# Moving the load, negation and accumulating load of one weight sum from unit 7 to unit 3 of a twenty-unit product schedule

## The chip, the cores and the metric

The kernel runs on one core of a Trainium2 chip. The metric is device time in microseconds (us) of one execution. The engines are TensorE (PE in the profile, with its weight loads as PEld), VectorE (DVE), ScalarE (ACT), GpSimd (POOL) and SyncE (SP); transfers are issued from SP, ACT and POOL.

## The reference, cut to what matters

`x` has 2708 rows of 1024 float32 values, `adj` is a 0/1 matrix of 2708 by 2708 in which a row has about four ones. One layer is computed:

```python
h = jnp.maximum(_layernorm(x, axis=-1), 0.0)
q = h @ W_q.T + b_q
k = h @ W_k.T + b_k
v = h @ W_v.T + b_v
z = (1 / sqrt(1024)) * (q @ k.T)
spare_z = z * adj
spare_z = jnp.where(spare_z == 0.0, -10000.0, spare_z)
attn = softmax(spare_z, axis=1)
x = x + relu(attn @ v)
```

## The kernel before, in words

**The algebra.** The kernel forms M = W_q.T W_k (scaled) once, and then needs only two products per row tile of 128 rows: `h M` (in place of the query), and `u W_v` where `u` is the weighted sum of the few rows of `h` that a row's neighbours name. Both products go in pairs of row tiles through a scheme of seven block products in place of eight. The 2 by 2 blocks of a 1024 by 1024 matrix lie in the tile `M[:, i, j]`, and sums of them in `T[:, 0..3]` (a view of `wlow`).

**The units.** There are twenty units, run in order by `multiply(n, ...)`: units 0 to 9 (kind "q") multiply by M, units 10 to 19 (kind "o") by W_v; one row tile (the last in `order`) is left for a single product at the end. `FIRST` is 4, `last_q` is 9. A unit has 28 matmuls of 512 columns, each shown as two instructions. Inside a unit, `after(i)` with i from 0 to 6 is called between the products, and everything else of the kernel is hung on these places: the steps written out in `steps_at` (a key (3, 5) is place 5 of unit 3), the next unit's operands, and the attention. The last two products of unit n lie on either side of `between(n)`, which calls `opened(n + 1)`: the first two products of the next unit and the copies `psy<-ps` (L1024) and `p<-ps` (L1029) of their sums on ScalarE. `u2` (L1060) is ScalarE's copy of the next sum.

**The blocks of M and of W_v.** In q units the first product that takes `s1` uses `T[:, 0]`, in o units `M[:, 0, 1]`. So `M[:, 0, 1]` (called `t1` in `after`) is free from the moment when the sums `T` and the squares of M are formed. It is to hold a sum of W_v for the o units: block (0, 0) of W_v is loaded into it, ScalarE negates it in two instructions, and an accumulating load on GpSimd's queue adds block (0, 1). At place 3 of unit 9 VectorE reads it for `T[:, 1]`.

**The squares.** `squared(k)` (L375) lets ScalarE sum the squares of M's block k, for a flag that chooses a general path after the main one. Steps `g0` to `g3` are the four blocks, `g4` is the bias row. Block 1 is `M[:, 0, 1]`.

**The neighbour table.** Each row's neighbours are found by VectorE and sorted by their count. `put` (steps `w`, L626) writes the table's rows in the sorted order to DRAM by one indirect transfer per row tile from GpSimd; `reload` (step `b`) brings them back. `w0-7` at (3, 6) writes the eight tiles that the attention takes first. `o0`, in `opened(4)`, sorts them (`pos_i`, L689).

**The attention.** From unit 4 on VectorE works a stream of scores (L863) and weighted sums (L923) over rows that GpSimd gathers by indirect transfers (`g<-h_dram`, L610; `pq`, L612). Its steps alternate by hand with what VectorE does for the units.

**What sets the order.** Up to the start of unit 4 the order on ScalarE and VectorE is as written (`manual_schedule`), from unit 4 on only that of VectorE; GpSimd, SP and TensorE are ordered by the compiler's planner, which lets an instruction go early when its inputs allow it. `tc.issue_after(ins)` puts what a block issues behind `ins` on that engine's queue. `load_rows` gathers the rows of a unit (`qr<-h_dram`, L612). `banks_for` (L760) puts the bias row into two accumulators.

Of the kernel before, what the change touches and what calls it, by code (L numbers as in the profile page):

```python
# [14 lines left out]
AF = mybir.ActivationFunctionType  # L15
ALU = mybir.AluOpType
AX = mybir.AxisListType

P = 128
NB = 512  # L20
# [3 lines left out]
SLOTS = 16  # L24
# [41 lines left out]
def tile_preln_masked_attention(  # L66
# [12 lines left out]
    nc = tc.nc  # L79
# [3 lines left out]
    scale = 1.0 / math.sqrt(D)  # L83
# [26 lines left out]
    h_dram = dram.tile([N, D], FT, name="h_dram")  # L110
# [65 lines left out]
    t = 0  # L176
    while t < NT:
# [4 lines left out]
        t = e  # L182
# [58 lines left out]
    def moments(t):  # L241

        group, xs, mv = next(g for g in normed.values() if t in g[0])
        i = t - group[0]
        junk = work.tile([P, D], mybir.dt.uint8, tag="junk", name="junk_x", bufs=1)
        nc.scalar.activation(junk, xs[i], AF.Copy, scale=-1.0 / (ROOT * D), accum_out=mv[:, i, 0:1])
        nc.scalar.activation(junk, xs[i], AF.Square, scale=1.0 / ROOT, bias=mv[:, i, 0:1], accum_out=mv[:, i, 1:2])
# [61 lines left out]
    def follow(steps):  # L309

        for step in steps.split():
            first, *only = step[1:].split(".")
            first, *last = first.split("-")
            first = int(first or 0)
            if step[0] == "s":
                stats(range(first, int(last[0] if last else first) + 1))
            elif step[0] == "m":
                moments(first)
            elif step[0] == "r":
                root(first)  # L320
            elif step[0] == "a":
                apply(first, *[range(int(o[0]), int(o[-1]) + 1) for o in only])
            elif step[0] in "hk":
                keep(first, step[0] == "h")
            elif step[0] == "+":
                owe(first)
            elif step[0] == "p":
                counted(first)
            elif step[0] == "c":
                counts(*halves[first])  # L330
            elif step[0] == "o":
                sorted_at.append(sort(*halves[first]))
            elif step[0] == "w":
                pooled.close()
                with tc.issue_after((behind if first < EARLY else products)[-1].ins):
                    entered.append(put(first, int(last[0]) + 1))
            elif step == "z":
                pooled.enter_context(tc.manual_schedule(engines={mybir.EngineType.Pool}))
                with tc.issue_after(entered[-1].ins):
                    reload(EARLY, NT)  # L340
            elif step[0] == "b":
                reload(*halves[first])
            elif step[0] == "g":
                squared(first)
            else:
                if step[0] == "e":
                    counted(first)
                if step[0] != "j":
                    found(first, *[range(int(o[0]), int(o[-1]) + 1) for o in only])
                if step[0] != "i":  # L350
                    listed(first)
# [94 lines left out]
    with tc.tile_pool(name="w", bufs=1, side="left") as wp:  # L446
# [11 lines left out]
        t1 = [work.tile([P, D], FT, tag="hT", name=f"t1_{k}", bufs=2) for k in range(2)]  # L458
# [49 lines left out]
        Y = [psum.tile([P, NB], FT, tag="tp", name=f"ps_y{i}") for i in range(H)]  # L508
# [98 lines left out]
    def gather(dst, src, t, w, n, skip=False):  # L607
        off = bass.IndirectOffsetOnAxis(ap=ptab.bitcast(U32)[:n, t, w:w + 1], axis=0)
        if skip:
            return nc.gpsimd.indirect_dma_start(out=dst, out_offset=None, in_=src, in_offset=off,  # L610
                                                bounds_check=N - 1, oob_is_err=False)
        return nc.gpsimd.indirect_dma_start(out=dst, out_offset=None, in_=src, in_offset=off)  # L612

    rows_of = {}
    FIRST = EARLY // 2
# [136 lines left out]

    placed = []

    def banks_for(row):

        return_ = []
        for h in range(NH):
            return_.append(psum.tile([P, NB], FT, tag="acc", name=f"ps{h}"))
            nc.scalar.copy(return_[h], row[:, h * NB:(h + 1) * NB])  # L760
        return return_

    def natural_rows(n):
# [23 lines left out]
    steps_ahead = {(1, 5): "o1"}  # L787

    slots, free = [], []
# [1 line left out]
    def searched():  # L791
        search.close()

        att = ph.enter_context(tc.tile_pool(name="att", bufs=1, side="right", reuse_waits="tile"))
        for i in range(HIGH):
            slots.append(att.tile([P, D], FT, name=f"g{i}"))

        assert len(adj_loads) == NT
# [210 lines left out]
    def add_block(bank, a, b, last=True):  # L1009
        for c in range(4):  # L1010
            mm = nc.tensor.matmul(bank, a[:, c, :], b[:, c, :], start=False, stop=(c == 3), skip_group_check=True)  # L1011
        return mm
# [3 lines left out]
    def opened(n):  # L1016

        if n not in banks_of:
            return
        X, Z = banks_of[n]  # L1020
        ops = ops_of[n][0]
        add_block(X, ops["a11"], M[:, 0, 0])
        Y = psum.tile([P, NB], FT, tag="acc", name="psy")
        nc.scalar.copy(Y, X)  # L1024
        if n == FIRST:
            follow("o0")
        products.append(add_block(Z, ops["s1"], T[:, 0] if units[n][0] == "q" else M[:, 0, 1]))
        p5 = small("p5")
        nc.scalar.copy(p5, Z)  # L1029
        opened_of[n] = Y, p5  # L1030

    def between(n):

# [16 lines left out]
    def multiply(n, results, after):  # L1050


        X, Z = banks_of.pop(n)
        ops = ops_of.pop(n)[0]
        Y, p5 = opened_of.pop(n)
        after(0)
        after(1)
        products.append(add_block(Y, ops["s2"], T[:, 1]))
        u2 = small("u2")
        nc.scalar.copy(u2, Y)  # L1060
        after(2)
        add_block(X, ops["a12"], M[:, 1, 0])
        results[0](X)
        after(3)
        products.append(add_block(Z, ops["s4"], M[:, 1, 1]))
        results[2](Z, u2)
        after(4)
        products.append(add_block(Y, ops["s3"], T[:, 2]))
        results[1](Y, p5)
        after(5)  # L1070
        between(n)
        add_block(Y, ops["a22"], T[:, 3])
        results[3](Y)
        after(6)
# [119 lines left out]
    def of_wv(i, j):  # L1194

        return wv[j][:, i * 4:(i + 1) * 4, :]
# [7 lines left out]
    def load_rows(unit):  # L1204
        kind, *pair = unit
        rows = []
        for t in pair:
            if t in held:
                rows.append(held.pop(t))
                continue  # L1210
            rows.append(row_tile(f"{kind}r_{t}"))
            if kind == "q":
                gather(rows[-1], h_dram[:, :], t, SLOTS, P)
            else:
                assert t in done, (t, done)
                if t in faced_tiles:
                    by_quarters(rows[-1], u_dram[t * P:(t + 1) * P, :])
                else:
                    nc.sync.dma_start(rows[-1], u_dram[t * P:(t + 1) * P, :])
        return rows  # L1220

    products = []
    last_q = len(q_pairs) - 1
# [13 lines left out]
    for n, unit in enumerate(units):  # L1237
# [15 lines left out]
        def after(i):  # L1253
# [15 lines left out]
                    with tc.issue_after(sorted_at[-1].ins):  # L1269
                        nc.vector.memset(g, 0.0)  # L1270
            b11, t1, b21, b22 = M[:, 0, 0], M[:, 0, 1], M[:, 1, 0], M[:, 1, 1]
            for at, place, src in (((-2, 0), t1, of_wv(0, 0)), ((0, 3), b21, of_wv(1, 0))):
                if (n - last_q, i) == at:
                    nc.sync.dma_start(place, src)
            if (n - last_q, i) == (0, 4):
                for h in range(2):
                    nc.scalar.copy(b22[:, 2 * h:2 * h + 2], T[:, 0, 2 * h:2 * h + 2])
            if (n - last_q, i) == (-2, 6):
                for h in range(2):
                    nc.scalar.activation(t1[:, 2 * h:2 * h + 2], t1[:, 2 * h:2 * h + 2], AF.Copy, scale=-1.0)  # L1280
                nc.gpsimd.dma_start(t1, of_wv(0, 1), accum_op=ALU.add)
            for at, place, a, b in (((0, 3), T[:, 1], T[:, 0], t1), ((1, 0), T[:, 2], T[:, 1], b11),
                                    ((1, 1), T[:, 3], b21, T[:, 1])):
                if (n - last_q, i) == at:
# [40 lines left out]
                follow(steps_at[n, i])  # L1325
            if (n, i) == (3, 4):
                searched()
            if (n, i) == (3, 6):
                for s in range(8, HIGH):
                    for c in range(0, D, D // 4):  # L1330
                        with tc.issue_after(entered[-1].ins):
                            nc.gpsimd.memset(slots[s][:, c:c + D // 4], 0.0)
# [70 lines left out]
    with tc.If(some > 0):  # L1403
# [19 lines left out]
        with tc.tile_pool(name="big", bufs=1, side="right") as big, tc.tile_pool(  # L1423
# [34 lines left out]
            with tc.For_i(0, NT) as i:  # L1458
                r0 = nc.snap(smin(i * P, N - P))
                rows = bass.ds(r0, P)  # L1460
# [119 lines left out]
```

## Time and profile before

| What | Before |
|---|---|
| time, median of 3 runs | 630.61 us (629.04 to 632.04) |
| time of the profiled execution | 627.51 us |
| its span, first to last instruction | 625.8 us, at a mean granted TensorE clock of 0.999 |
| TensorE | 618.9 us busy, 99% of the span |
| VectorE | 526.4 us, 84% |
| GpSimd | 366.9 us, 59% |
| ScalarE | 290.4 us, 46% |
| weight loads of TensorE | 310.0 us, 50% |
| transfers | 183.24 MB, 293 GB/s on average |

How to read it: shares are over the whole span, and the stages differ. The first 107 us form M, the normed rows and the neighbour lists, units 0 to 3 run to about 217 us beside the search, and the attention begins at about 239 us. A row of the timeline gives start, duration, engine, line, operation, output and input, and in square brackets the idle time of the engine just before it and what ended it. POOLq, SPq and ACTq are the issues of transfers in an engine's queue.

### The profile page before, as it was taken

To read this page: it belongs to the slowest core of one execution; us is meant where nothing else is said; L and a number is where in the kernel's file an instruction comes from. 1 tells how busy PE (TensorE), PEld (TensorE's weight loads), DVE (VectorE), ACT (ScalarE), POOL (GpSimd) and SP (SyncE) were. 2 spreads that over 40 slices of the span, in tenths; PEclk is the share of its full clock that TensorE was granted. 3 is DMA by queue.
4 is the path that set the end of the run, shared out by engine and by line. 5 is a ranking of instruction groups with operands and counts; after the bars stand their busy time and mean duration, and the time that the engine had idled before them with its cause. 6 is when DMAs were issued, how large, how long until landed. Compare 5 with 4: busy or idle time off the path is not lost.

```text
span 625.8 us, 6069 instructions
## 1 busy us (share of the span) xinstructions
PE 618.9 (99%) x1571; PEld 310.0 (50%) x1571; DVE 526.4 (84%) x1024; ACT 290.4 (46%) x421; POOL 366.9 (59%) x394
## 2 busy tenths in 40 slices
PE   9999999999999999999999999999999999999996
PEld 5777767444444444444444444444444444444442
DVE  5999878988988947979898998999988899898541
ACT  3538985749677372433331532443442433432300
POOL 2649870786668577856654342767577657752421
PEclk9999999999999999999999999999999999999999
DMA  8999998688797559997696999999999999995571
GB/s 331 407 369 323 340 356 317 211 265 322 251 369 278 171 166 364 349 321 250 212 374 193 368 340 311 282 332 328 347 341 343 335 306 340 293 293 139 149 254 71
DMA packets 65952, 183.24 MB, mean 293 GB/s; under 512 B 10055, under 2 KB 20631, under 8 KB 65272
## 3 DMA queue, kind: packets, MB, share of 16 engines
q0 software_dynamic: 26656, 86.02, 43.8%
q1 hardware_dynamic: 32026, 71.53, 32.7%
q10 hardware_dynamic: 7230, 25.25, 10.4%
q8 instruction: 14, 0.23, 0.1%
q14 instruction: 26, 0.21, 0.1%
HBM read 147.23 MB, written 43.88 MB: 305 GB/s over the span
## 4 chain that ended last, share of the span: by engine, by line
PE 99%; POOL 0%; DVE 0%; POOLq 0%; issue 0%
PE ps L1011 46%; PE psy L1011 33%; PE ps_y L476 7%; PE ps_x L476 4%; PE ps_z L476 4%; PE pt L415 3%; PE ps_y L511 1%; PE ps_h L1230 0%; PE ps_v L594 0%; DVE y_alone L1396 0%; POOL out_dram L1380 0%; POOLq L1402 0%; POOL hsum L121 0%; PE ps_in L678 0%; PE ps_all L680 0%
## 5 line engine op out<-in xcount | busy, mean ns | idle before, releaser
L610 POOL DMA_INDIRECT g<-h_dram,tab x93 | 120.0, 1290 | 60.6 <-issue 20.0
L1011 PE MATMUL ps<-M,a 128*128 128x512 f32 x320 | 144.0, 593 | 0.0
L1011 PE MATMUL psy<-wlow,s 128*128 128x512 f32 x320 | 143.9, 592 | 0.0
L863 DVE SCALAR_TENSOR_TENSOR junk<-g,pq 128x1024 uint8<-128x1024 f32 x92 | 112.3, 1220 | 9.6 <-DMA g<-h_dram,tab 7.9
L1011 PE MATMUL ps<-M,s 128*128 128x512 f32 x240 | 107.9, 592 | 0.0
L1011 PEld LDWEIGHTS ps<-M,a 128*128 128x128 f32 x320 | 60.0, 190 | 72.2 <-issue 71.3
L1011 PEld LDWEIGHTS psy<-wlow,s 128*128 128x128 f32 x320 | 60.0, 190 | 72.1 <-issue 70.6
L923 DVE SCALAR_TENSOR_TENSOR u<-g,coef,u 128x1024 f32<-128x1024 f32 x70 | 89.8, 1283 | 7.0 <-ACT u L912 5.6
L389 DVE FIND_INDEX8 at<-ones,adj 128x8 uint32<-128x685 f32 (+1 forms) x88 | 74.5, 864 | 0.0
L1011 PEld LDWEIGHTS ps<-M,s 128*128 128x128 f32 x240 | 45.5, 190 | 57.2 <-issue 56.5
L1011 PE MATMUL psy<-wlow,a 128*128 128x512 f32 x160 | 72.0, 593 | 0.0
L368 ACT ACTIVATE sized<-adj 128x2708 uint8<-128x2708 f32 (+1 forms) x22 | 54.2, 2466 | 7.3 <-DMA adj<-in_adj_dram 6.0
L298 POOL TENSOR_TENSOR hsum<-hsum,x 128x256 f32<-128x256 f32 (+1 forms) x56 | 38.7, 732 | 26.5 <-DVE wlow L444 22.4
L1115 POOL DMA_INDIRECT y<-in_x_dram,tab x19 | 32.6, 1714 | 32.2 <-ACT y L1132 16.6
L1011 PEld LDWEIGHTS psy<-wlow,a 128*128 128x128 f32 x160 | 30.3, 190 | 38.6 <-issue 37.1
L808 POOL DMA_INDIRECT out_dram<-y,tab x21 | 27.0, 1284 | 16.0 <-issue 13.9
L1011 PE MATMUL ps<-wlow,s 128*128 128x512 f32 x80 | 36.1, 593 | 0.0
L944 ACT COPY v<-u 128x1024 f32<-128x1024 f32 x20 | 20.9, 1044 | 32.3 <-DVE u L923 24.8
L912 ACT ACTIVATE u<-g,coef 128x1024 f32<-128x1024 f32 x16 | 18.4, 1148 | 28.8 <-DVE coef L911 23.5
L626 POOL DMA_INDIRECT tab_dram<-tab,pos_i x22 | 21.6, 982 | 13.7 <-DVE pos_i L689 8.2
L276 ACT ACTIVATE x<-x,r 128x1024 f32<-128x1024 f32 (+1 forms) x22 | 25.8, 1232 | 5.1 <-POOL r L266 5.1
L760 ACT COPY ps<-bp_sb 128x512 f32<-128x512 f32 x42 | 24.6, 595 | 7.7 <-DVE y L1150 7.0
(253 smaller groups left out, 841.1 us busy)
## 6 DMA issues: line engine op xcount, KB each, us to landing
adj<-in_adj_dram SPq DMA_DIRECT2D x21, 1354.0 KB, 11.1
x<-in_x_dram SPq DMA_DIRECT2D x21, 512.0 KB, 11.0
h_dram<-x ACTq DMA_DIRECT2D x21, 512.0 KB, 7.2
u_dram<-v ACTq DMA_DIRECT2D x20, 512.0 KB, 7.3
or<-u_dram SPq DMA_DIRECT2D x80, 128.0 KB, 10.0
q_late<-q SPq DMA_DIRECT2D x12, 512.0 KB, 5.6
pq<-q_late POOLq DMA_DIRECT2D x12, 512.0 KB, 10.2
M<-in_wv_dram SPq DMA_DIRECT2D x3, 1024.0 KB, 15.9
```

The costliest lines, as they stand in the source:

```text
L276: nc.scalar.activation(xs[i][:n], xs[i][:n], AF.Relu, bias=r[:n, 4, i:i + 1], scale=r[:n, 3, i:i + 1])
L298: small.append(nc.gpsimd.tensor_add(hsum[:n, cols], hsum[:n, cols], xt[:n, cols]))
L368: nc.scalar.activation(sized[:n], a[:n, :, :PW], AF.Abs, accum_out=total[:n, t:t + 1])
L389: nc.vector.max_index(at[:n, k - first_k, g, :], ones[:n, 0:8], a[:n, g, :])
L476: mm = nc.tensor.matmul(bank, a_tile(o + H * a[0], a[1], i), b(o), start=first and o == 0, stop=(o == H - 1), skip_group_check=True)
L610: return nc.gpsimd.indirect_dma_start(out=dst, out_offset=None, in_=src, in_offset=off, bounds_check=N - 1, oob_is_err=False)
L760: nc.scalar.copy(return_[h], row[:, h * NB:(h + 1) * NB])
L808: to = nc.gpsimd.indirect_dma_start(out=out, out_offset=bass.IndirectOffsetOnAxis(ap=ptab.bitcast(U32)[:n, t, SLOTS:SLOTS + 1], axis=0), i ...
L863: chained(lambda: nc.vector.scalar_tensor_tensor(junk, g_of[t][s], 1.0, tq[t], op0=ALU.mult, op1=ALU.mult, accum_out=zall[:, t, s:s + 1]))
L923: chained(lambda: nc.vector.scalar_tensor_tensor(u, g_of[t][s], coef[:, s:s + 1], u, op0=ALU.mult, op1=ALU.add))
L1011: mm = nc.tensor.matmul(bank, a[:, c, :], b[:, c, :], start=False, stop=(c == 3), skip_group_check=True)
L1115: return nc.gpsimd.indirect_dma_start(out=y[:n], out_offset=None, in_=x, in_offset=off, compute_op=ALU.add)
```

## The change

The three steps on `t1` that stood at (7, 0) and (7, 6) go to unit 3. The load of block (0, 0) is issued by ScalarE at (3, 2), behind its copy `u2` of unit 3, in place of SP. The negation stands at (3, 5), behind ScalarE's copies for the accumulators, and the accumulating load of block (0, 1) is issued by GpSimd behind the latest gather of `load_rows`, which is written ahead of the puts `w0-7` at (3, 6). So that the block is free by then, its squares (`g1`) go from (3, 6) into `opened(3)`, behind the copy `p5`; `g0` goes from (3, 5) to (3, 6). The lists `bank_at`, `rows_at` and `copied_at` only keep the instructions for `issue_after`. Nothing else is changed; no arithmetic is added or removed.

```diff
@@ banks_for
+    bank_at, rows_at, copied_at = [], [], []
-            nc.scalar.copy(return_[h], row[:, h * NB:(h + 1) * NB])
+            bank_at.append(nc.scalar.copy(return_[h], row[:, h * NB:(h + 1) * NB]))
@@ steps_at
-                (3, 1): "i21", (3, 3): "p21", (3, 4): "j21 c0", (3, 5): "g0", (3, 6): "w0-7 g1 g2 g3 g4", (4, 4): "b0"}
+                (3, 1): "i21", (3, 3): "p21", (3, 4): "j21 c0", (3, 6): "w0-7 g0 g2 g3 g4", (4, 4): "b0"}
@@ opened(n), behind the copy p5
+        if n == FIRST - 1:
+            follow("g1")
@@ multiply
-        nc.scalar.copy(u2, Y)
+        copied_at.append(nc.scalar.copy(u2, Y))
@@ load_rows
-                gather(rows[-1], h_dram[:, :], t, SLOTS, P)
+                rows_at.append(gather(rows[-1], h_dram[:, :], t, SLOTS, P))
@@ after(i)
-            for at, place, src in (((-2, 0), t1, of_wv(0, 0)), ((0, 3), b21, of_wv(1, 0))):
-                if (n - last_q, i) == at:
-                    nc.sync.dma_start(place, src)
+            if (n - last_q, i) == (0, 3):
+                nc.sync.dma_start(b21, of_wv(1, 0))
...
-            if (n - last_q, i) == (-2, 6):
-                for h in range(2):
-                    nc.scalar.activation(t1[:, 2 * h:2 * h + 2], t1[:, 2 * h:2 * h + 2], AF.Copy, scale=-1.0)
-                nc.gpsimd.dma_start(t1, of_wv(0, 1), accum_op=ALU.add)
...
+            if (n, i) == (3, 2):
+                with tc.issue_after(copied_at[-1].ins):
+                    nc.scalar.dma_start(t1, of_wv(0, 0))
+            if (n, i) == (3, 5):
+                with tc.issue_after(bank_at[-1].ins):
+                    for h in range(2):
+                        nc.scalar.activation(t1[:, 2 * h:2 * h + 2], t1[:, 2 * h:2 * h + 2], AF.Copy, scale=-1.0)
+                with tc.issue_after(rows_at[-1].ins):
+                    nc.gpsimd.dma_start(t1, of_wv(0, 1), accum_op=ALU.add)
```

## The prediction

> **What bounds the kernel now.** I read the page's head first, then the waits of TensorE, then the chain that ended last, and at the end the timelines of each queue around units 3 and 4.
>
> ```profile
> span 625.8 us, 6069 instructions
> PE 618.9 (99%) x1571; PEld 310.0 (50%) x1571; DVE 526.4 (84%) x1024; ACT 290.4 (46%) x421; POOL 366.9 (59%) x394
> PE 99%; POOL 0%; DVE 0%; POOLq 0%; issue 0%
> ```
>
> TensorE is busy for 618.9 of 625.8 us, and the chain that ended last is TensorE alone. The next fences show where the other 6.9 us lie: first three stretches of the span (each engine's busy time and instructions, clock, share of the transfer engines, GB/s), then all waits of TensorE (total, times, longest), then pieces of the chain (start, duration, instructions).
>
> ```profile
> 1.20:620.00 618.80, 618.80 (x1571) 309.95 (x1571) 525.49 (x1023) 290.35 (x421) 365.31 (x388) 1.00 0.88 295
> 620.00:625.80 5.80, 0.08 (x1) 0.00 (x0) 0.69 (x1) 0.00 (x0) 0.96 (x1) 0.88 0.24 90
> ```
>
> ```profile
> PE ps_y L511 <- POOL hsum L121: 1.2, 1, 1.2
> ```
>
> ```profile
> 187.39 6.87 PE psy L1011 x16
> 209.87 3.59 PE ps L1011 x8
> 368.13 7.08 PE psy L1011 x16
> 592.39 6.87 PE ps L1011 x16
> ```
>
> TensorE's only wait is the 1.2 us before its first instruction. From 1.20 to 620.00 us it has no idle time, and the 5.8 us behind it are the last addition and scatter, which the change does not touch. The chain's pieces say that this busy time is not waiting in disguise: 16 instructions take 6.87 us (0.43 us each) at 187 us as at 592 us; the slow pieces are 209.87 (3.59 for 8, where 3.44 is the rule) and 368.13 (7.08 for 16), some 0.1 to 0.2 us each. The granted clock in the first stretch is 1.00. So the kernel is as long as TensorE's own instructions, and an edit that leaves those alone can gain a few tenths of a us. It can lose only where it makes TensorE wait. That is the question for each part: how late may what it moves become before TensorE stands still?
>
> **The change part by part.** The rows for ScalarE, which carries most of it (start, duration, what, and idle time before it):
>
> ```profile
> 187.43 0.58 ACT L1029 COPY p<-ps 128x512 f32<-128x512 f32 x1 [1.35 <-PE ps L1011]
> 190.86 0.58 ACT L1105 COPY q<-psy 128x512 f32<-128x512 f32 x1 [2.85 <-PE psy L1011]
> 196.40 0.57 ACT L1060 COPY u<-psy 128x512 f32<-128x512 f32 x1
> 197.73 0.58 ACT L1094 COPY q<-ps 128x512 f32<-128x512 f32 x1 [0.77 <-PE ps L1011]
> ...
> 205.91 0.58 ACT L718 COPY a<-pt 128x512 f32<-128x512 f32 x1 [3.14 <-PE pt L415]
> 206.39 1.06 ACT L375 ACTIVATE junk_m<-M 128x1024 uint8<-128x1024 f32 x1
> ...
> 208.54 0.19 ACT L375 ACTIVATION_READ_ACCUMULATOR junk_m<-M 128x1 f32 x1
> 209.78 0.57 ACT L1024 COPY psy<-ps 128x512 f32<-128x512 f32 x1 [1.06 <-PE ps L1011]
> ...
> 231.97 2.00 ACT L1280 ACTIVATE M<-M 128x1024 f32<-128x1024 f32 x2 [3.76 <-DMA M<-in_wv_dram]
> 233.88 0.57 ACT L1081 COPY taken<-psy 128x512 f32<-128x512 f32 x1
> ...
> 250.75 0.33 ACTq L946 DMA_DIRECT2D u_dram<-v  x1
> ```
>
> 1. *Squares of block 1* (`g1`). Their cost is that of `g0`, from 206.39 to 208.73 (208.54 + 0.19): 2.34 us. They go behind `p<-ps`, which ends at 188.01, ahead of `q<-psy`, which waits 2.85 us for TensorE until 190.86. 188.01 + 2.34 = 190.35, so they lie wholly in that gap, with 0.5 us to spare. Cost 0. Without the cover, 2.34 us would fall on the copy of a result, which nobody needs at once.
>
> 2. *Issue of the load by ScalarE.* An issue of ScalarE's queue took 0.33 us, the same load by SP 0.52 us (its row below). It stands behind `u<-psy`, which ends at 196.97, in a gap of 0.77 us. By either price it fits. Cost 0; the load starts at about 197.0. On SP it goes away at 226.56, where the next store stands behind it; nobody on the chain waits for that store.
>
> 3. *The negation* costs 2.00 us (row 231.97) and takes the place of `g0`, 2.34 us, at 206.39; `g0` goes to the four squares at (3, 6), whose number stays (`g1` left them). So ScalarE's load there falls by 0.34 us, if the block has landed by 206.39. Behind the negation stands `psy<-ps` at 209.78, and behind that all of ScalarE: this is the wait that the change adds. Landing is bounded by these rows:
>
> ```profile
> 225.44 0.38 SPq L638 DMA_DIRECT2D tab<-tab_dram  x1
> ...
> 226.56 0.52 SPq L1274 DMA_DIRECT2D M<-in_wv_dram  x1
> ```
>
> ```profile
> DMA to landing us min/median/max: 12.3/14.1/15.9
> ```
>
> ```profile
> q0 software_dynamic: 208, 0.73, 56.4%
> ```
>
> ```profile
> 201.00:202.00 1.00, 1.00 (x10) 1.00 (x9) 0.78 (x2) 1.00 (x3) 1.00 (x2) 1.00 0.00 0
> ```
>
> The same megabyte, issued at 226.56, let the negation go at 231.97: 5.4 us. The slowest landing of any transfer into M took 15.9 us (second fence, min, median, max). From 197.0 that is 202.4 or 212.9. I take 202.4 and a little: in the four us from 197 the gathers' queue moves only 0.73 MB (third fence: packets, MB, share), and from 201 to 202 us the transfer engines do nothing at all (fourth: share 0.00), so 1 MB has room. I put the landing at 203, 3 us ahead of need. [...] The upper bound is rival A.
>
> The load also shares the transfer engines with the two gathers for unit 4, issued from 193.51 on, whose rows TensorE turns at these times:
>
> ```profile
> 200.96 1.04 PE L415 MATMUL pt<-ident,qr 128*128 128x128 f32 x8
> ...
> 205.27 1.04 PE L415 MATMUL pt<-ident,qr 128*128 128x128 f32 x8
> ...
> 217.60 3.60 PE L1011 MATMUL psy<-wlow,s 128*128 128x512 f32 x8
> ```
>
> Both gathers are in by 201 (share 0.00 from there). The first is half of their 1 MB and, being first in its queue, is nearly through when the load's first bytes come; the second may lose some 2 us, and has from about 200.5 to 205.27. Cost 0; without the cover, up to 2 us of TensorE.
>
> 4. *The accumulating load* on GpSimd's queue, and the queue that it is moved past:
>
> ```profile
> 208.13 1.06 POOL L612 DMA_INDIRECT qr<-h_dram,tab  x1 [0.31 <-issue]
> 214.30 1.01 POOL L626 DMA_INDIRECT tab_dram<-tab,pos_i  x1 [5.12 <-DVE pos_i L689]
> ...
> 223.28 0.97 POOL L626 DMA_INDIRECT tab_dram<-tab,pos_i  x1 [0.30 <-issue]
> ...
> 228.78 0.99 POOL L612 DMA_INDIRECT pq<-q_dram,tab  x1 [1.43 <-DMA tab<-tab_dram]
> ...
> 258.54 1.02 POOL L1281 DMA_DIRECT2D M<-in_wv_dram  x1
> ```
>
> It takes 1.02 us and 0.3 between issues. GpSimd stands idle for 5.12 us before the first put, which waits for VectorE's `pos_i`; the negation ends at about 208.4, the last gather at 209.19, so the issue is over by about 210.5, 3.8 us before 214.30. Cost 0, and 1.3 us less among the gathers at 258. In the shared queue its data go ahead of the puts'. It landed 12.3 us after issue among gathers (the minimum above); from 209.5 that gives 221.8, before the last put is even issued (223.28). So the reload at 225.44 stays where it is; if the data took as much again, the reload and the attention would be about 8 us later (233.8 less 225.4).
>
> 5. *What becomes better at 226 to 270 us.* The load's 1 MB leaves the engines just when the first `pq` and `g` gathers are asked for, and ScalarE no longer stands 3.76 us in front of `taken`. VectorE gets its first score sooner:
>
> ```profile
> 238.87 1.23 DVE L863 SCALAR_TENSOR_TENSOR junk<-g,pq 128x1024 uint8<-128x1024 f32 x1 [3.47 <-DMA g<-h_dram,tab]
> ...
> 252.25 1.28 DVE L722 TENSOR_TENSOR s<-a,pt 128x512 f32<-128x512 f32 x2 [1.06 <-ACT a L718]
> ```
>
> ```profile
> 261.43 3.60 PE L1011 MATMUL ps<-wlow,s 128*128 128x512 f32 x8
> ```
>
> The gathers may come 1 to 3 us earlier (at most the 3.47 us that the first score waited). But even now what VectorE makes at 252.25 is used by TensorE at 261.43, about 8 us after the first of the pair is done. Nothing on the chain waits for the attention, so the gain is put at 0.
>
> The sum: 0 + 0 + 0 + 0 + 0 = 0 on the profiled execution's 627.51 us (625.8 of span and 1.7 around it). That execution lies 3.1 us under the median of 630.61; my forecast is the median unchanged, 630.6, of itself 629.0 to 632.0 as the runs shown spread. What a measurement of this kernel tells from no change is about 0.5%, 3.15 us.
>
> **The rivals.**
>
> *A. The load comes late and TensorE waits (slower).* Place: ScalarE's queue at 206.39, where the negation holds up `psy<-ps`. That copy opens the sum to which TensorE adds at 217.60. With 2.00 for the negation and 0.57 for the copy, it decides from a landing at 215.0 on, 18 us after issue; from there each us costs one. For it: in this stage no load has been issued from ScalarE's queue before, the gathers share the engines, and two of three such transfers needed 12.3 and 15.9 us. Against it: even 15.9 leaves 2.1 us. If the delay were 24 us (half as much again as 15.9), the stall would be 5.9 us: 636.5.
>
> *B. TensorE's busy time hides waits (faster).* [...] Against it stands the even 0.43 us per instruction, early and late, which bounds the gain within the profile by about 1 us. What the profile can't exclude is that the 3.1 us between it and the median are such waits in the gathering stage; if all went, the time would be 627.5.
>
> *C. The change doesn't do what it says.* GpSimd is ordered by the planner; it may let the puts pass if it reckons the negation late. Then the accumulating load comes at about 224, among or behind the puts, and issue 1.3 us is added before `pq`. Against the 8 us at 252.25 this is nothing: 630.6 too.
>
> **How the numbers follow.** No change to the chain: 0.76. C: 0.05, the same time. A: 0.12, the margins being 2 us at the worst row and 12 us at the likeliest, but the order of a whole stage is moved. B: 0.07. Faster by over 0.5% only if B takes all of the 3.1 us, 0.07; within 0.5%: 0.81; slower: 0.12. The range goes down to B's 627.5 and up into A as far as a stall of about 4 us, 634.5, which leaves out A's longer stalls and lesser odds.
>
> **What would show it.** Right: TensorE again with the one wait of 1.2 us and 618.9 us; squares of one block at about 188; the load from ScalarE's queue at 197; the negation at 206 to 209 with no wait for a transfer before it; the accumulating load at about 209.5, the first put still at 214.3 and the reload at about 225.4; the first score at 236 to 239. Wrong: a wait of ScalarE for `M<-in_wv_dram` that runs past 215, TensorE waiting for `psy` at 217 or for `qr` at 201, puts that start after 216, or a TensorE whose busy time falls.

## The result, and the profile after

| What | Before | After |
|---|---|---|
| time, median of 22 runs each | 629.93 us (628.32 to 634.25) | 632.98 us (630.46 to 635.71) |
| ratio after to before, 95% interval | | 1.0042 (1.0030 to 1.0054) |
| time of the profiled execution | 627.51 us | 631.25 us |
| its span, mean granted TensorE clock | 625.8 us, 0.999 | 629.5 us, 0.995 |

The changed kernel is 0.42% slower by the ratio, which is not taken from the medians; these lie 3.05 us apart. That is less than the 0.5% that the prediction took as the limit of a measurement, but with 22 runs on each side the interval does not contain 1: there is a loss, and the forecast of no change was wrong.

The head of the page of the changed kernel, and below it all waits of TensorE in it (total, times, longest, in us):

```profile
span 629.5 us, 6070 instructions
PE 620.0 (98%) x1571; PEld 311.0 (49%) x1571; DVE 526.0 (84%) x1024; ACT 292.4 (46%) x421; POOL 369.6 (59%) x394
PE 95%; DMA 3%; ACT 1%; issue 0%; POOL 0%; DVE 0%; POOLq 0%
```

```profile
PE pt L415 <- DMA qr<-h_dram,tab: 2.5, 1, 2.5
PE ps_y L511 <- POOL hsum L121: 1.2, 1, 1.2
```

TensorE has one wait that it did not have: for `qr`, the gathered rows of unit 4. The span grew by 3.7 us; this wait is 2.5 of it, and TensorE's busy time grew by the other 1.1 (620.0 against 618.9) though it runs the same 1571 instructions. Why it grew is seen in the timeline of TensorE in the changed kernel (start, duration, what, instructions, idle time before it):

```profile
203.24 1.77 PE L415 MATMUL pt<-ident,qr 128*128 128x128 f32 x8 [2.55 <-DMA qr<-h_dram,tab]
204.80 4.62 PE L1013 MATMUL psy<-wlow,s 128*128 128x512 f32 x8
209.26 1.04 PE L415 MATMUL pt<-ident,qr 128*128 128x128 f32 x8
210.13 3.60 PE L1013 MATMUL ps<-M,a 128*128 128x512 f32 x8
```

and in three stretches of 3.41 us, the middle one from the clock's fall to its rise (busy time and instructions of PE, PEld, DVE, ACT, POOL, then granted clock, share of the transfer engines, GB/s):

```profile
200.02:203.43 3.41, 0.86 (x4) 0.23 (x3) 3.34 (x7) 1.22 (x2) 3.41 (x6) 1.00 1.00 406
203.43:206.84 3.41, 3.41 (x11) 2.38 (x10) 3.07 (x18) 2.82 (x4) 3.41 (x6) 0.50 0.34 139
206.84:210.25 3.41, 3.41 (x15) 1.90 (x15) 1.93 (x7) 0.36 (x1) 2.64 (x4) 1.00 0.29 58
```

Behind the 2.55 us of waiting the granted clock is 0.50 for 3.41 us, and then 1.00 again. The eight turns take 1.77 us where they took 1.04, the eight matmuls behind them 4.62 where the ones at 210.13 take 3.60: 0.73 + 1.02 = 1.75 us for the clock. In the kernel before the two groups of turns stood at 200.96 and 205.27; here they stand at 203.24 and 209.26. So TensorE is 2.28 us later at the first and 3.99 at the second, and the span ends 3.7 later: nothing behind 210 us adds to it, and a little is won back.

The transfers in that place, from the timelines of ScalarE and GpSimd in the changed kernel and from its queues between 197 and 201 us (packets, MB, share of the 16 transfer engines; the same stretch of before showed 0.73 MB of the gathers' queue `q0`):

```profile
194.50 0.35 ACTq L1329 DMA_DIRECT2D M<-in_wv_dram  x1
196.95 0.57 ACT L1064 COPY u<-psy 128x512 f32<-128x512 f32 x1
```

```profile
196.59 1.08 POOL L612 DMA_INDIRECT qr<-h_dram,tab  x1 [5.53 <-DMA h_dram<-x]
```

```profile
q10 hardware_dynamic: 136, 1.04, 61.5%
q1 hardware_dynamic: 173, 0.56, 34.7%
q0 software_dynamic: 27, 0.11, 6.7%
```

The load's megabyte is issued at 194.50, 2.5 us ahead of the copy `u<-psy` behind which it is written: the issue did not wait for that copy. Its 1.04 MB then take the stretch in which the gathers moved 0.73 MB before; they move 0.11. But a second thing differs between the two profiles: the first gather is issued at 196.59, where before it was at 193.51. The experiments had to tell the two apart.

### The profile page after: what moved, and what is told of

It reads as the page before. It is cut to its first block, busy times and chain, and to the rows that moved or that the text cites. A ratio compares the mean times of both kernels' runs of the same rounds, so it can differ in the third digit from the quotient of the medians.

```text
span 629.5 us, 6070 instructions
## 1 busy us (share of the span) xinstructions
PE 620.0 (98%) x1571; PEld 311.0 (49%) x1571; DVE 526.0 (84%) x1024; ACT 292.4 (46%) x421; POOL 369.6 (59%) x394
## 4 chain that ended last, share of the span: by engine, by line
PE 95%; DMA 3%; ACT 1%; issue 0%; POOL 0%; DVE 0%; POOLq 0%
PE ps L1013 44%; PE psy L1013 31%; PE ps_y L476 7%; PE ps_x L476 4%; PE ps_z L476 4%; PE pt L415 3%; DMA h_dram<-x 2%; DMA qr<-h_dram,tab 1%; PE ps_y L511 1%; ACT x L276 0%; ACT sized L368 0%; PE ps_h L1234 0%; PE ps_v L594 0%; DVE y_alone L1404 0%; POOL out_dram L1388 0%
## 5 line engine op out<-in xcount | busy, mean ns | idle before, releaser
L610 POOL DMA_INDIRECT g<-h_dram,tab x93 | 121.8, 1310 | 61.9 <-issue 20.4
L476 PE MATMUL ps_y<-wlow 128*128 128x512 f32 x64 | 27.6, 592 | 0.0
```

Of the source, the lines that this page charges most:

```text
L476: mm = nc.tensor.matmul(bank, a_tile(o + H * a[0], a[1], i), b(o), start=first and o == 0, stop=(o == H - 1), skip_group_check=True)
```

## Experiments

**Theory 1**: the load's megabyte falls into transfer engines that are already full (share 1.02 from 190 to 194 us in the changed kernel, ahead of the load), unit 4's gather lands later, and TensorE waits for `qr` and then runs slower. **Theory 2**: ScalarE's own work, the squares and the issue, delays the row stores or copies on which the gather waits. **Theory 3**: the early negation and accumulating load disturb what follows. "Issue to turn" below is from the issue of the first gather to TensorE's first turn of its rows. Each run of kernels was timed beside the kernel before on the same chip.

### The two kernels again

The first profile of before lay 2.4 us under that kernel's median, so both kernels were run and profiled again, with no edit.

> The changed kernel itself once more, as the yardstick for the others on this chip and to see whether its profile shows the same wait. Both theories: 0.3 to 0.5% over before, 1.9 to 3.2 us. Theory 1 (transfers): the load's 1 MB shares full transfer engines with the gathers of unit 4's rows, which land after TensorE is due to turn them; TensorE waits 0.5 to 3 us for qr at about 200 us in the profile and runs at a lower clock for a few us behind that (mean clock 0.993 to 0.998). Theory 2 (ScalarE): what ScalarE has more to do makes its stores of the rows late, so the gathers are issued late (at 196.6 us in the one profile so far, against 193.5 before) whatever the load does; the wait for qr is then there too, with the gathers issued at 195 us or later.

Measured: 631.99 us, ratio 1.0037 (1.0022 to 1.0052). Its profile waits 3.13 us for `qr`, with the first gather issued at 197.07 and the turn at 203.78.

> The kernel before itself once more, for a second profile of it and as a measure of what the comparison can tell: ratio 1.000 within 0.15%. Theory 1 in its present form says that the one profile shown before was taken on an execution at the fast end (627.5 us against a median of 629.6 to 630.6) in which ScalarE was not held up at 170 to 179 us; an ordinary execution of it has the copy q<-ps of unit 2 at 177 us or later, the gathers issued at 195 us or later, and TensorE waiting 0 to 2 us for qr, at a clock of 0.998 or more. If the profile shows the gathers at 193.5 again and no wait for qr, the extra 2 us of the median are somewhere else.

Measured: 629.26 us, ratio 0.9987 (0.9967 to 1.0007), and a profile of 628.2 us. The kernel before in this second profile, first TensorE's waits and then rows of its timelines:

```profile
PE pt L415 <- DMA qr<-h_dram,tab: 1.2, 1, 1.2
...
PE psy L1011 <- ACT psy L1024: 1.0, 1, 1.0
```

```profile
172.02 0.58 ACT L718 COPY a<-pt 128x512 f32<-128x512 f32 x1 [2.43 <-remote]
177.80 0.58 ACT L1094 COPY q<-ps 128x512 f32<-128x512 f32 x1 [2.74 <-PE ps L1011]
...
183.03 0.34 ACTq L283 DMA_DIRECT2D h_dram<-x  x1
197.16 1.08 POOL L612 DMA_INDIRECT qr<-h_dram,tab  x1 [5.67 <-DMA h_dram<-x]
201.83 1.06 PE L415 MATMUL pt<-ident,qr 128*128 128x128 f32 x8 [1.20 <-DMA qr<-h_dram,tab]
```

In the first profile of before the same rows read:

```profile
173.70 0.58 ACT L1094 COPY q<-ps 128x512 f32<-128x512 f32 x1 [0.68 <-PE ps L1011]
180.39 0.34 ACTq L283 DMA_DIRECT2D h_dram<-x  x1
193.51 1.08 POOL L612 DMA_INDIRECT qr<-h_dram,tab  x1 [2.70 <-DMA h_dram<-x]
```

So the kernel before itself has the late gather: here ScalarE's copy at 177.80 waits 2.74 us instead of 0.68, the row store behind it is issued at 183.03 instead of 180.39, and the gather, which waits for the stores, at 197.16 instead of 193.51. Every other profile of an unexchanged order issues it between 196 and 199. The first profile was the exception, and it alone had hidden that TensorE already waits 1.2 us for `qr`. The late gather is not the change's doing. The time from there on is: 201.83 − 197.16 = 4.7 us from issue to turn before, 6.65 and 6.7 in the two profiles after. Between 197 and 201 us the gathers move 0.54 MB in this profile of before, and 0.11 beside the load. What delays ScalarE at 170 to 179 us (the trace names "remote" as the releaser of the first) stays open.

### The load behind the gathers, all else as changed

```diff
-                with tc.issue_after(copied_at[-1].ins):
-                    nc.scalar.dma_start(t1, of_wv(0, 0))
+                late = nc.sync.dma_start(t1, of_wv(0, 0))
+                tc.add_manual_dep(late.ins, rows_at[1].ins.name, ...)   # unit 4's second gather
```

> The changed kernel, but the load of block (0, 0) is issued by SP and waits until both gathers of unit 4's rows have landed; squares, negation and accumulating load as in the change. Theory 1 (the load delays the gathers): within 0.1% of before, no wait of TensorE for qr, load issued at about 200.5 us and landed by 205, negation at about 206.4. Theory 2 (ScalarE's own added work): still 0.3 to 0.5% slower than before, the wait for qr still there. Theory 3 (negation and accumulating load at the early place cost): still 0.3 to 0.5% slower, with the wait somewhere behind 206 us.

Measured: 629.11 us, ratio 0.9994 (0.9981 to 1.0007). The timelines of GpSimd, TensorE, SP and ScalarE in this kernel:

```profile
197.37 1.08 POOL L612 DMA_INDIRECT qr<-h_dram,tab  x1 [6.96 <-DMA h_dram<-x]
203.22 1.06 PE L415 MATMUL pt<-ident,qr 128*128 128x128 f32 x8 [1.92 <-DMA qr<-h_dram,tab]
```

```profile
204.37 0.33 SPq L1328 DMA_DIRECT2D M<-in_wv_dram  x1
...
210.83 2.01 ACT L1335 ACTIVATE M<-M 128x1024 f32<-128x1024 f32 x2 [2.05 <-DMA M<-in_wv_dram]
```

The whole loss is gone with this one transfer 10 us later (204.37 for 194.50), while squares, negation and accumulating load stand as changed. That refutes theory 3 and the part of theory 2 that lies in the squares. The turns take 1.06 us behind a wait of 1.92: no lower clock. The negation now waits 2.05 us for the block and still nobody waits for it.

### The squares alone

Only `g1` and `g0` are moved; load, negation and accumulating load stand as in the kernel before. The planner lets the load go as soon as its block is free:

```diff
-                (3, 5): "g0", (3, 6): "w0-7 g1 g2 g3 g4"
+                (3, 6): "w0-7 g0 g2 g3 g4"        # and follow("g1") in opened(3)
```

> Of the change only the squares' new place; the load stays with SP, where the planner now lets it go at about 192 us, ahead of the gathers. Theory 1: the megabyte is in front of the gathers instead of beside them on engines that are full until 200 us, so the wait for qr is there too: 0.2 to 0.6% slower than before. Theory 2 (ScalarE's queue): the load is no longer issued by ScalarE and its ring holds only the stores, so 0 to 0.2% slower than before, by the squares alone.

Measured: 632.38 us, ratio 1.0045 (1.0029 to 1.0062). The timelines of SP, GpSimd and TensorE in this kernel:

```profile
193.93 0.48 SPq L1278 DMA_DIRECT2D M<-in_wv_dram  x1
197.35 1.08 POOL L612 DMA_INDIRECT qr<-h_dram,tab  x1 [6.50 <-DMA h_dram<-x]
...
204.19 1.06 PE L415 MATMUL pt<-ident,qr 128*128 128x128 f32 x8 [2.75 <-DMA qr<-h_dram,tab]
```

With the block free early the planner put the load on SP at 193.93, so this kernel became the transfer by itself from another queue, and it costs as much as the whole change, with no issue by ScalarE: theory 2 has fallen. Issue to turn is 6.84 us with SP's issue of the load and 6.65 with ScalarE's.

### Half of the load

```diff
-                    nc.scalar.dma_start(t1, of_wv(0, 0))
+                    nc.scalar.dma_start(t1[:, 0:2], of_wv(0, 0)[:, 0:2])
+                late = nc.sync.dma_start(t1[:, 2:4], of_wv(0, 0)[:, 2:4])   # behind the gathers
```

> The changed kernel, but only half of block (0, 0), 0.5 MB, is loaded by ScalarE at the early place; the other half is issued by SP and waits for the gathers of unit 4's rows. Theory 1: the gathers lose about half as much, so TensorE waits less or not at all: 0 to 0.25% slower than before. Theory 2 and 3: as the changed kernel, 0.3 to 0.5% slower.

Measured: 631.07 us, ratio 1.0019 (1.0003 to 1.0034): by the ratio about half the loss for half the bytes, but the interval still touches that of the whole load (1.0022 to 1.0052). Issue to turn was 5.5 us, between the 4.7 to 5.9 of the kernels without an early load so far and the 6.65 to 6.84 with a whole one. The wait in this profile was 2.78 us, because its gather was issued late even for this kernel (198.66).

### The rows of unit 4 stored earlier

Step `p17` goes behind `a8 k8`, so that the row stores for unit 4, and with them the gathers, come sooner. Tried on before, on after, and on the kernel with the late load:

```diff
-                (2, 3): "p17 a8 k8 z"
+                (2, 3): "a8 k8 p17 z"
```

> The kernel before, with only the order of two steps of place 3 of unit 2 changed: ScalarE normalises and stores the last three row tiles (a8 k8) ahead of its sum over an adjacency tile (p17), so the stores start up to 2.7 us earlier and the planner puts the next adjacency load behind them. Theory 1: the gathers of unit 4's rows are issued 2 us earlier or more, any wait for qr goes, 0.1 to 0.4% faster than before (down to 627.5 us, where the fast executions are). If unit 4's rows are not what holds TensorE in ordinary executions: no change within 0.1%.

Measured: 632.49 us, ratio 1.0040 (1.0019 to 1.0061).

> The changed kernel with the same two steps exchanged. Theory 1: the gathers are again 2 to 3 us earlier and get their bytes before or beside the load with time to spare, so most of the change's loss goes: between 0.3% faster and 0.15% slower than before, no or a short wait for qr. If the loss came from anything else in the change than the rows of unit 4: still 0.3 to 0.5% slower.

Measured: 633.77 us, ratio 1.0059 (1.0033 to 1.0085).

> The kernel whose load waits for the gathers (load_wait), with the same two steps exchanged. Theory 1: as rows_first_before, 0.1 to 0.4% faster than before, no wait for qr, since the load is out of the gathers' way in either order. If the load's early place helps by itself: faster than rows_first_before by 0.1% or more; my expectation is that it does not.

Measured: 630.05 us, ratio 1.0001 (0.9984 to 1.0019).

The gathers were issued some 5 us sooner (191.92, 191.52 and 192.74), and the wait for `qr` shrank to 0.47 us or to nothing. The rows came hardly sooner: in the exchanged before TensorE turns them at 200.98, after that wait, 9.1 us behind the issue. No kernel gained. TensorE's waits in the exchanged before, then VectorE's from 190 to 215 us in it:

```profile
PE ps_in L678 <- DVE sort L666: 1.8, 1, 1.8
...
PE ps L1011 <- DVE s L722: 1.0, 1, 1.0
PE pt L415 <- DMA qr<-h_dram,tab: 0.5, 1, 0.5
```

```profile
DVE at L389 <- DMA adj<-in_adj_dram: 8.9, 2, 4.5
```

The last loads of `adj` are what became late: VectorE stands 8.9 us for them, 3.4 us in the second profile of before, and its sums and the sort reach TensorE late. In the exchanged after, whose profiled execution lies 3.7 us above its median, TensorE waits 8.0 us at once:

```profile
PE psy L1013 <- DVE q L1101: 8.0, 1, 8.0
```

So what the gathers gained the loads of `adj` lost; the exchange turned the wait into a new one. The kernel with the late load has the same new waits as the exchanged before, and is still not slower. Its waits of TensorE:

```profile
PE ps_in L678 <- DVE sort L666: 1.7, 1, 1.7
...
PE ps L1013 <- DVE s L722: 1.0, 1, 1.0
```

The two kernels part behind these waits, as their stretches show (columns as above; first the exchanged before, then the exchanged kernel with the late load):

```profile
209.09:212.50 3.41, 1.38 (x5) 0.30 (x3) 3.06 (x18) 1.09 (x3) 0.00 (x0) 1.00 0.87 281
212.50:215.92 3.42, 2.59 (x3) 1.18 (x4) 3.34 (x7) 0.00 (x0) 0.00 (x0) 0.50 0.27 108
215.92:219.33 3.41, 3.41 (x5) 1.35 (x4) 2.93 (x7) 0.00 (x0) 1.16 (x2) 0.50 0.00 0
```

```profile
208.34:211.75 3.41, 1.68 (x5) 0.40 (x4) 3.03 (x20) 2.28 (x3) 0.99 (x1) 1.00 0.96 299
211.75:215.17 3.42, 2.39 (x7) 1.15 (x8) 3.36 (x7) 0.00 (x0) 0.00 (x0) 1.00 1.11 399
```

TensorE stood for 2.86 us in the one (1.83 and 1.03, with two short matmuls between) and for 2.76 in the other; the clock fell to 0.50 for 6.83 us in the one and stayed at 1.00 in the other. The stretches are as long as the lower clock in the changed kernel, 3.41 us; in the exchanged before they end where the clock falls (212.50) and where it rises (219.33). In the one that ends at the fall TensorE stood for 2.03 us (3.41 less 1.38 busy); in the other kernel it stood for 1.73 us in one stretch and 1.03 in the next. Whether this division is what kept the clock up there was not shown. The lower clock is worth some 3 us: the eight matmuls behind the second wait take 6.67 us in the one and 3.70 in the other. That accounts for these two profiled executions (spans of 632.0 and 628.7 us), but not for the medians: six of the ten executions of the exchanged before have a mean clock of 0.997 or 0.998, as profiles with no lowered clock have, and still a median of 632.25 us. What is slow in those stays open.

### Other bytes out of the way

Two stores of unit 2 (`q_dram`, 0.5 MB each, tiles 4 and 5) lie in the same stretch, and nothing needs them soon. They are made to wait for unit 4's gathers, in the kernel before, in the changed kernel, and in the changed kernel with its load held back too:

```diff
-            (nc.scalar if t < 4 else nc.sync).dma_start(dst, q)
+            stored = (nc.scalar if t < 4 else nc.sync).dma_start(dst, q)
+            if t in (4, 5):
+                tc.add_manual_dep(stored.ins, rows_at[1].ins.name, ...)
```

> The kernel before, but the two stores of unit 2's results (tiles 4 and 5, 0.5 MB each, issued by SP at about 184.5 and 191 us) wait until both gathers of unit 4's rows have landed; they are read only from 228 us on. Theory 1 (whatever bytes stand in front of the gathers delay them): 1 MB less ahead of or beside the gathers brings them 1 to 2.5 us earlier, the wait of TensorE for qr (1.2 us in the second profile of before) goes, 0.1 to 0.3% faster than before. Against it: the two exchanged steps brought the gathers 5 us earlier and were not faster, because the last adjacency load then came late; here that load gets earlier too, so no wait for it. If TensorE's wait for qr is not what the ordinary executions lose: within 0.1% of before.

Measured: 628.00 us, ratio 0.9983 (0.9965 to 1.0001). The gathers did not come earlier (the first is issued at 197.94), and TensorE still waits 1.59 us for `qr` in the profile; so why the median is lower was not shown.

> The changed kernel with the same two stores held back. Theory 1: the load's 1 MB then stands in place of the stores' 1 MB, so it should be about as fast as before: between 0.15% faster and 0.15% slower, wait for qr 0 to 2 us. If only the load's queue or place matters and not the number of bytes in front: still 0.3 to 0.5% slower.

Measured: 629.54 us, ratio 1.0005 (0.9990 to 1.0021). The time came out as expected: with a megabyte of stores taken out where the load put one in, the changed kernel is as long as before. That the bytes are the reason is argued, for the profiled execution doesn't show it: its time, 633.78 us, is 4.2 above the median, it waits 3.75 us for `qr`, and issue to turn is 6.5 us, as with load and stores together. It is one of four executions of twelve with a mean clock of 0.996 or less.

> The changed kernel with the load and the two stores all held back until the gathers have landed, the load behind the stores on SP. Theory 1: no wait for qr, as fast as stores_wait_before (0.1 to 0.3% faster than before); the load lands at about 206 to 208 us, so the negation may wait for it a us or two, which delays no product. If the early sum of W_v is worth something by itself (less traffic in the gathering stage): faster than stores_wait_before by 0.1% or more, which I do not expect.

Measured: 627.49 us, ratio 0.9973 (0.9958 to 0.9988), the one kernel here whose interval lies wholly below 1. Its profile has a span of 625.9 us. Its load and its negation, and those of TensorE's waits that lie behind its first instruction:

```profile
203.58 0.78 SPq L1332 DMA_DIRECT2D M<-in_wv_dram  x1
...
211.13 2.01 ACT L1339 ACTIVATE M<-M 128x1024 f32<-128x1024 f32 x2 [4.59 <-DMA M<-in_wv_dram]
```

```profile
PE pt L415 <- DMA qr<-h_dram,tab: 0.5, 1, 0.5
PE psy L1013 <- DVE q L1105: 0.2, 1, 0.2
```

The wait for `qr` is down to 0.5 us. How much of this gain is the late stores alone and how much the moved sum cannot be told: the interval overlaps that of the late stores in the kernel before.

## Why the prediction was wrong, step by step

**What bounds it: right, from an execution that was not ordinary.** TensorE's busy time is the bound, and only a wait could cost. But "TensorE's only wait is the 1.2 us before its first instruction" holds for that one execution. The second profile of the kernel before has 1.2 us for `qr` and 1.0 for `psy`, and 628.2 − 625.8 = 2.4 us of span is these and a wait of 0.2. The prediction saw that its profile lay 3.1 us under the median and did not ask which cover was thinner in an ordinary execution.

**1, the squares: right.** From the timeline of ScalarE in the changed kernel:

```profile
189.20 1.05 ACT L375 ACTIVATE junk_m<-M 128x1024 uint8<-128x1024 f32 x1
...
191.34 0.19 ACT L375 ACTIVATION_READ_ACCUMULATOR junk_m<-M 128x1 f32 x1
191.44 0.57 ACT L1109 COPY q<-psy 128x512 f32<-128x512 f32 x1
```

2.33 us from first to last. They start 1.2 us later than foreseen (189.20 against 188.01), so the 0.5 us to spare was not there: the copy behind them is 0.6 us later than before, which nobody waits for.

**2, the issue: wrong by 2.5 us.** The load was to start at about 197.0, behind `u<-psy`; it was issued at 194.50, ahead of it. This brought its bytes in front of the gathers' instead of behind the first.

**3, the negation: right; the load beside the gathers: the step that failed.** The negation started behind `a<-pt` and waited for no transfer, and the copy `psy<-ps` behind it waited for TensorE only:

```profile
210.38 2.01 ACT L1333 ACTIVATE M<-M 128x1024 f32<-128x1024 f32 x2
213.82 0.57 ACT L1026 COPY psy<-ps 128x512 f32<-128x512 f32 x1 [1.44 <-PE ps_in L678]
```

What failed is "The first is half of their 1 MB and, being first in its queue, is nearly through when the load's first bytes come", and with it "Cost 0; without the cover, up to 2 us of TensorE". It rests on a gather issued at 193.51 and a load issued at 197.0. In ordinary executions the gather is issued near 197 and the load at 194.50: the order is the reverse. The share of 0.00 at 201 to 202 that was to show room was read from that same execution; in the changed kernel the share is 1.00 from 200.02 to 203.43. The term measured 1.4 us more waiting than in the second profile of before (2.55 less 1.20), near to the "up to 2 us" that had been named as the price without the cover. The prediction had no term for what followed: 1.75 us of lower clock. Together 3.1 us, against 3.05 between the medians. Of single profiles that is no proof: those two spans differ by 1.3 us, since the second of before has 1.2 us of other waits that the changed kernel lacks. What shows the cause is the loss that went when the load alone was held back.

The clocks of all executions say the same. Profiles with a stretch of lower clock behind a wait have a mean clock of 0.992 to 0.996, those without one 0.997 to 1.000. Of 90 executions of the kernel before that were timed beside the experiments, 23 have 0.996 or less; their median is 631.32 us, that of the others 629.13. Of the changed kernel's 34 executions 29 have it, with 633.01 us against 630.46; with the load behind the gathers it is one of 12, with the squares alone nine of nine. By that mark the clock falls in a quarter of the executions of before, and with the load's megabyte in most; behind which wait it fell, a mean does not say.

A wait of 2.55 us was enough to lower the clock, and those of 1.20, 1.59 and 1.92 us were not: behind these three the eight turns took 1.06 us and the eight matmuls 3.60. In the changed kernel the stretch of lower clock is 3.41 us long, from 203.43 to 206.84.

**4, the accumulating load: right in its order.** It is issued behind the last gather and ahead of the first put, which still waits for VectorE; both are later by some 2 to 3 us, with TensorE, and so is the reload (227.79 against 225.44). A sum in that part is off by a little: a landing twice as late, counted from 209.5, is at 234.1, not 233.8. The rows of GpSimd:

```profile
212.69 0.99 POOL L1335 DMA_DIRECT2D M<-in_wv_dram  x1 [0.51 <-ACT M L1333]
216.66 1.04 POOL L626 DMA_INDIRECT tab_dram<-tab,pos_i  x1 [2.98 <-DVE pos_i L689]
```

**5, the attention: right only beside TensorE.** The first score stands at 241.09 us, 2.2 later than before and past the 236 to 239 that was named as a sign. TensorE is 4.0 later by then: a relative gain of 1.8 us, inside the estimate of 1 to 3, and the end of the kernel does not feel it.

```profile
241.09 1.23 DVE L865 SCALAR_TENSOR_TENSOR junk<-g,pq 128x1024 uint8<-128x1024 f32 x1 [3.26 <-DMA g<-h_dram,tab]
```

**The rivals.** A had the direction and the shared engines, but the wrong victim: it let the gathers delay the load, with the wait behind ScalarE's negation at 217, where the load delays the gathers and TensorE waits for these at 203. That wait had a price in part 3 and a place among the signs of being wrong, but no rival and no chance of its own. B's suspicion that the 3.1 us between profile and median held waits of the gathering stage fits the second profile of before and the clocks above, but the change added to them and took none away. C did not occur.

## What to carry to other kernels

Where the transfer engines are full, as they were here (a share of 0.99 to 1.07 from 190 to 203 us in the changed kernel), moving a load earlier moves it in front of something: find which gather lands in that stretch and who waits for it, and hold the load behind that gather by a dependency on it. A cover that is read from one profiled execution is only as good as that execution is ordinary; where it lies under the median, ask of each cover of 1 to 3 us whether it still stands in a later one. Price a new wait of the bounding engine with the lower clock behind it, not with its length alone: here that was another 1.7 or 3.0 us.

## What the runs showed of the hardware that was not expected

- An issue on ScalarE's queue that is written behind a copy ran 2.5 us ahead of it (194.50 against 196.95): being written behind the copy held back nothing where the load had no need of the copy's data. Whether the compiled order or the engine let it pass, the trace does not show.
- In the stretches shown the granted clock is 1.00 or 0.50. In the changed kernel it is 0.50 from 203.43 to 206.84 us, behind a wait of 2.55 us, and again from 626.68 us, behind the last matmul. Waits for `qr` of 1.20, 1.59 and 1.92 us left the turns and matmuls behind them at their usual times; those of 2.55 us and more did not. Two waits of 2.86 us in sum lowered the clock for 6.83 us in the exchanged before, two of 2.76 us left it at 1.00 in the exchanged kernel with the late load. What sets the limit, and how waits that lie close together count, was not shown.
- The lower clock cost 1.7 to 1.8 us behind waits of 2.55, 2.75 and 2.78 us, and 3.0 us behind 3.13 and 3.75 us. That is what the eight turns and the eight matmuls behind them took beyond 1.04 and 3.60 us: 1.77 and 4.62 behind 2.55 us, 1.94 and 5.69 behind 3.13 us.
- The first gather's rows came 6.5 to 6.8 us after their issue where a whole megabyte was loaded at the same time, from either of the two queues tried, and 4.5 to 5.9 us after it where none was (gathers issued at 196 to 199 us).
